# Transposing softmax blocks inside their own rows, and letting the value matmuls read them there

## The chip, the cores and the metric

The kernel runs on one core of one Trainium2 chip. The metric is the device time of one launch in microseconds; a kernel's figure is the median of its runs. The engines of the core go by the names of the profile: PE (TensorE matmuls) and PEld (its weight loads), DVE (VectorE), ACT (ScalarE), POOL (GpSimd), SP (SyncE, which issues the DMAs here).

## The reference

One residual layer of multi-query attention on 64 sequences ("images" below) of 128 tokens and 512 features, 16 heads of 64, one key and one value head shared by all. Everything is fp32.

```python
xn = layernorm(x, g_in)                                  # x: 64 x 128 x 512
q  = (xn @ Wq).reshape(b, n, 16, 64).transpose(0, 2, 1, 3) * 64 ** -0.5
k, v = split(xn @ Wkv)                                   # 64 wide each
k, v = [null_k; k], [null_v; v]                          # a null key in front: 129 keys
sim  = einsum('bhid,bjd->bhij', q, k) + bias             # bias 16 x 128 x 128
sim  = where(causal or masked, -max, sim)
attn = softmax(sim)
out  = einsum('bhij,bjd->bhid', attn, v)
out  = layernorm(out.reshape(b, n, 1024) @ Wo, g_out)
return x + out
```

## The kernel before

The work goes image by image (`b` from 0 to 63) in a software pipeline whose order is written out by hand: the order in the program is the order on each engine, and a step `n` runs parts of several images. Steps alternate between `step_a` (even `n`) and `step_b` (odd `n`); each ends with `region(n)`. Two steps make one round. The last five images go through `last_step` and `last_region`, which do the same with fewer parts.

**The softmax rows.** `S[b]` is one tile of 128 partitions by 8 slots by 194 words (`ROW = 1 + 64 + 128 + 1`). The 128 query rows of the 16 heads are folded by the causal mask: a partition quadrant of 32 rows holds, in each of its 8 slots, 64 columns for a query block that can see at most two key blocks of 32 (`LK`, columns 1 to 64) and 128 columns for one that can see up to four (`UK`, columns 65 to 192). Column 0 and column 193 belong to the null key. So the keys of each slot start at word 1 of a row of 194 words, an odd word in every slot.

An image's rows go through these operations, all of them in place in `S[b]`:

- `bias_add` (L526, POOL): allocates `S[b]` from the pool `sp` and writes bias plus mask, 1552 words a partition.
- `scores_add` (L573, DVE): adds the scores that PE left in PSUM (`heads`, L542).
- `scores_max` (L578, DVE), `exps` (L587, ACT), `rinv` (L604, DVE), `scale` (L608, POOL): the softmax of the two halves.
- `blocks_T` (L623, DVE): a transpose of the 32x32 blocks, 48 of them side by side on each quadrant, into the tile `sb` (6 blocks x 8 slots x 32 words, packed; one buffer in the pool `hp`).
- `values` (L654, PE): 32 matmuls, whose moving operand is read from `sb` and whose weights are the values `vr`. A matmul covers 32 rows and 64 output columns of the array, so eight of them (four quadrants by two column halves) fill it. Eight of the matmuls read two blocks of 4 slots (256 columns) and twenty-four read one (128 columns). In `sb` the 4 slots of a block lie behind one another: 128 words in one run.

fp32 matmuls appear in the profile as two records each, so an image has 64 records of L654.

**Who waits for whom around it.** With two buffers of `S`, `bias_add(n + 2)` takes the buffer of image `n`, whose last reader is `blocks_T(n)`, at the end of `region(n - 1)`. With one buffer of `sb`, `blocks_T(n + 1)` must come after `values(n)`. The order at the end of a step is

```python
    def region(n):
        ...            # scores_lower(nb), scores_one(nb, 1)            PE
        values(n)      #                                                PE
        ...            # scores_add, scores_max, scores_add             DVE
        values_out(n)  #                                                ACT
        blocks_T(n+1)  #                                                DVE
```

In `step_a` the next `bias_add` is the first thing on POOL after that; behind it in POOL's queue stand `pair_pow` (L784) and `scale` (L608). In `step_b` it comes late, behind `out_sums` and a `scale`.

The rest of PE's work in a step is the query projection (L488), the output projection (L738, L685) and the keys and values (L359); L488 and L738 are written as seven products of halves in place of eight.

Of the kernel before, what the change touches and what calls it, by code (L numbers as in the profile page):

```python
# [8 lines left out]
FP = mybir.dt.float32  # L9
# [8 lines left out]
def kernel(  # L18
# [59 lines left out]
    nc = tc.nc  # L78
# [3 lines left out]
    P = 128  # L82
# [7 lines left out]
    Q = 32  # L90
    NQ = P // Q
    NF = NC // 2
    R8 = 2 * NF
    NL = DH
    ROW = 1 + NL + N + 1
# [172 lines left out]
    mneg = const.tile([P, GB, ROW], FP, name="mneg")  # L268
    nc.gpsimd.memset(mneg[:, :, 0 : ROW : ROW - 1], 0.0)

    sp = ctx.enter_context(tc.tile_pool(name="sp", bufs=2))
    bp = ctx.enter_context(tc.tile_pool(name="bp", bufs=2))
    hp = ctx.enter_context(tc.tile_pool(name="hp", bufs=2))
    small = ctx.enter_context(tc.tile_pool(name="small", bufs=4))
# [237 lines left out]
    S, nmax, rsum = {}, {}, {}  # L512
# [106 lines left out]

    def blocks_T(b):  # L620

        sb = hp.tile([P, 6, R8, Q], FP, tag="sb", name=f"sb_{b}", bufs=1)
        nc.vector.transpose(  # L623
            sb.rearrange("p j e q -> p e j q"),
            S[b][:, :, 1 : ROW - 1].rearrange("p e (j k) -> p e j k", k=Q),
        )
        sbs[b] = sb

    pos = {}
# [221 lines left out]
    def region(n):  # L851
        nb, eb = n + 2, n + 1
        if nb < B:
            scores_lower(nb)
            scores_one(nb, 1)
        if n >= 0:
            values(n)
        if nb < B:
            scores_add(nb, 0)
            scores_max(nb, 0)  # L860
            scores_add(nb, 1)
            late_max.append(nb)
        if n >= 0:
            values_out(n)
        if 0 <= eb < B:
            blocks_T(eb)

    def last_region(n):
        nb, eb = n + 2, n + 1
        if nb < B:  # L870
            scores_one(nb, 0)
            scores_add(nb, 0)
        values(n)
        if nb < B:
            scores_max(nb, 0)
        values_out(n)
        if eb < B:
            blocks_T(eb)
        if nb < B:
            scores_one(nb, 1)  # L880
            scores_add(nb, 1)
            late_max.append(nb)
# [404 lines left out]
    q_half(7, 1)  # L1287
    weight_sum(3)
    blocks_T(0)
    for n in range(-1, P_LAST + 4):  # L1290
        step(n)
# [51 lines left out]
```

## Time and profile before

| | |
|---|---|
| Runs | 1071.23, 1072.93, 1073.17 us; median 1072.93 us |
| Span of the profiled execution | 1069.6 us |
| Busy, share of the span | PE 99%, PEld 83%, DVE 75%, POOL 65%, ACT 64% |
| Granted TensorE clock | 0.998 of full, mean over the span |

The profile gives the profiled execution by its span, from its first instruction to its last; no other time of that execution is listed. The median of the runs is 3.33 us more than this span, and the runs lie 1.6 to 3.6 us above it: what lies around the span (launch and end) is taken to be that, for both kernels. A line name such as L654 is a line of the kernel before. The changed kernel is two lines shorter from L624 on, so its L652 is L654 here.

### The profile page before, as it was taken

The page shows a single profiled execution, that of the slowest core. Times are in us where ns is not written, and L with a number is a line of the kernel's source. Part 1 is how long each engine was busy: PE and PEld are TensorE (multiplying, and loading weights), DVE is VectorE, ACT ScalarE, POOL GpSimd, SP SyncE. Part 2 cuts the span into 40 slices and gives each one's busy share as a digit, 9 for nine tenths or more (in the row PEclk, how much of TensorE's full clock was granted, in tenths as well). Part 3 has the DMA queues.
Part 4 walks back from the last instruction along what each step waited for, and adds up shares of the span by engine and source line. Part 5 has one row for each costly group of instructions (what it writes and reads, how often), then busy time and mean ns, then how long its engine had stood idle before and what let it go on. Part 6 is the DMA issues. An engine that isn't in the chain of part 4 may idle for free.

```text
span 1069.6 us, 31102 instructions
## 1 busy us (share of the span) xinstructions
PE 1055.3 (99%) x12272; PEld 883.4 (83%) x12272; DVE 806.0 (75%) x1676; ACT 679.3 (64%) x2748; POOL 695.3 (65%) x520
## 2 busy tenths in 40 slices
PE   8999999999999999999999999999999999999997
PEld 7877888888888888888888888888888888888653
DVE  5766787787878778787787877788787787666672
ACT  2565666676666666666766666766766766655682
POOL 3586667675775857667675775857667675765562
PEclk9999999999999999999999999999999999999999
DMA  6633414234241333314234141343313333101211
GB/s 209 168 107 93 131 49 129 73 102 139 75 124 52 129 105 102 118 48 135 83 103 139 53 138 57 107 130 99 113 54 125 94 103 120 50 32 46 66 61 70
DMA packets 68690, 105.11 MB, mean 98 GB/s; under 512 B 8640, under 2 KB 32832, under 8 KB 66752
## 3 DMA queue, kind: packets, MB, share of 16 engines
q1 hardware_dynamic: 67440, 102.08, 30.8%
q8 instruction: 96, 1.57, 0.7%
q10 hardware_dynamic: 1104, 1.05, 0.3%
q14 instruction: 50, 0.41, 0.1%
HBM read 67.45 MB, written 35.65 MB: 96 GB/s over the span
## 4 chain that ended last, share of the span: by engine, by line
PE 92%; DMA 4%; DVE 1%; ACT 1%; POOL 1%; issue 0%; SPq 0%; DVEq 0%; ACTq 0%
PE pa L488 19%; PE pyX L738 18%; PE pc L488 10%; PE pyY L738 9%; PE ps L542 9%; PE po L654 8%; PE pkv L359 6%; PE py L685 5%; PE pw L488 5%; PE pyw L738 4%; DMA x<-in_x_dram 2%; PE pq L437 1%; ACT oT L671 1%; DMA wq<-in_L_cond_Wq_dram 1%; DMA gin<-in_L_cond_g_in_dram 0%
## 5 line engine op out<-in xcount | busy, mean ns | idle before, releaser
L587 ACT ACTIVATE s<-s,nmax 128x65 f32<-128x65 f32 (+1 forms) x1024 | 372.0, 370 | 3.1 <-DVE nmax L578 3.1
L526 POOL TENSOR_TENSOR s<-biasp,mneg 128x1552 f32<-128x1552 f32 x64 | 206.1, 3221 | 159.8 <-DVE sb L623 151.9
L608 POOL TENSOR_TENSOR s<-s,rinv 128x512 f32<-128x512 f32 (+1 forms) x128 | 190.3, 1487 | 109.3 <-DVE rinv L604 109.3
L587 ACT ACTIVATION_READ_ACCUMULATOR s<-s,nmax 128x1 f32 x1024 | 198.2, 194 | 0.0
L671 ACT ACTIVATE oT<-po,nv 128x256 f32<-128x256 f32 x256 | 100.2, 474 | 153.9 <-PE po L654 153.8
L738 PE MATMUL pyX<-wT,oT 128*128 128x256 f32 x672 | 161.7, 383 | 0.0
L573 DVE TENSOR_TENSOR s<-ps,s 128x256 f32<-128x256 f32 (+2 forms) x188 | 125.1, 691 | 36.2 <-PE ps L542 36.2
L738 PEld LDWEIGHTS pyX<-wT,oT 128*128 128x128 f32 x672 | 123.5, 190 | 22.5 <-issue 2.7
L578 DVE TENSOR_REDUCE nmax<-s 128x8 f32<-128x520 f32 (+1 forms) x128 | 122.4, 956 | 2.4
L488 PE MATMUL pa<-xS,wq 128*128 128x256 f32 x480 | 123.2, 379 | 0.0
L623 DVE STREAM_TRANSPOSE sb<-s 128x1536 f32<-128x1536 f32 x64 | 113.3, 1770 | 4.7 <-POOL s L608 4.5
L542 PEld LDWEIGHTS ps<-kT,qT 64*64 64x64 f32 x4096 | 87.1, 134 | 26.2 <-issue 11.5
L542 PE MATMUL ps<-kT,qT 64*64 64x64 f32 (+1 forms) x4096 | 104.6, 248 | 1.5 <-DVE s L573 1.5
L488 PEld LDWEIGHTS pa<-xS,wq 128*128 128x128 f32 x480 | 91.2, 190 | 12.4
L654 PE MATMUL po<-sb,vr 32*64 32x128 f32 (+1 forms) x4096 | 91.3, 305 | 0.0
L654 PEld LDWEIGHTS po<-sb,vr 32*64 32x64 f32 x4096 | 70.8, 130 | 16.8 <-issue 10.7
L509 DVE TENSOR_TENSOR qT<-pc,ku 128x256 f32<-128x256 f32 x120 | 49.6, 413 | 42.5 <-ACT ku L499 31.6
L506 ACT COPY qT<-pa 128x256 f32<-128x256 f32 x60 | 22.3, 371 | 89.1 <-PE pa L488 89.1
L499 ACT COPY ku<-pa 128x256 f32<-128x256 f32 x120 | 44.7, 372 | 51.9 <-PE pa L488 50.0
L359 PE MATMUL pkv<-wkv,xT 128*128 128x128 f32 x512 | 71.8, 285 | 1.9 <-DVE kvt L374 1.9
L359 PEld LDWEIGHTS pkv<-wkv,xT 128*128 128x128 f32 x512 | 65.9, 195 | 8.7 <-issue 5.0
L718 POOL TENSOR_TENSOR yS<-oT 128x512 f32<-128x512 f32 x28 | 35.6, 1271 | 53.6 <-ACT oT L671 53.6
(95 smaller groups left out, 1957.2 us busy)
## 6 DMA issues: line engine op xcount, KB each, us to landing
x<-in_x_dram SPq DMA_DIRECT2D x64, 256.0 KB, 5.0
res<-in_x_dram SPq DMA_DIRECT2D x64, 256.0 KB, 6.2
out_dram<-y SPq DMA_DIRECT2D x64, 256.0 KB, 2.4
xd<-xb SPq DMA_DIRECT2D x14, 1024.0 KB, 4.0
xT<-xd SPq DMA_DIRECT2D x56, 256.0 KB, 5.9
vr<-vd SPq DMA_DIRECT2D x64, 128.0 KB, 2.7
kT<-kd SPq DMA_DIRECT2D x64, 64.0 KB, 1.9
kd<-kb SPq DMA_DIRECT2D x16, 128.0 KB, 2.6
```

The lines of the kernel that those rows point to most:

```text
L359: nc.tensor.matmul(pkv, xT[g][:, t, kc, :], wkv[:, kc, :], start=(kc == 0), stop=(kc == KC - 1),)
L488: nc.tensor.matmul(prod[tag], w[:, kc, f * P : (f + 1) * P], t[:, :, kc, :], start=(start and kc == 0), stop=(kc == HK - 1), skip_group_ch ...
L526: nc.gpsimd.tensor_tensor(S[b], biasp, mneg[:, t].unsqueeze(1).broadcast_to([P, R8, ROW]), ALU.add,)
L542: nc.tensor.matmul(to[r][i * DH : (i + 1) * DH, f, :], qT[g][rows, f, t, NQ - 1 - i if hf else i], kT[g][rows, 0 : NQ if hf else NQ // 2, ...
L573: nc.vector.tensor_tensor(sv, ps, sv, ALU.add)
L578: nc.vector.tensor_reduce(nmax[b][:, hf], S[b][:, :, WITH_NULL[hf]], AX.X, ALU.max, negate=True)
L587: nc.scalar.activation(row, row, AF.Exp, bias=nmax[b][:, hf, k : k + 1], accum_out=rsum[b][:, hf, k : k + 1],)
L608: nc.gpsimd.tensor_tensor(sv, sv, rinvs.pop((b, hf)).unsqueeze(2).broadcast_to([P, R8, sv.shape[2]]), ALU.mult,)
L623: nc.vector.transpose(sb.rearrange("p j e q -> p e j q"), S[b][:, :, 1 : ROW - 1].rearrange("p e (j k) -> p e j k", k=Q),)
L654: nc.tensor.matmul(po[s][rows, half], vr[g][quad(s), j, t, :], sb[quad(s), slots, r * NF : (r + 1) * NF, :], start=slots is first, stop=Tr ...
L671: nc.scalar.activation(oT[b][:, u * NF : (u + 1) * NF, :].rearrange("p f (i q) -> p i f q", i=NQ)[:, blocks], po, AF.Identity, bias=nv2,)
L738: nc.tensor.matmul(prod[key], h[:, c, :], w[:, c, :], start=(start and c == 0), stop=(c == HC - 1), skip_group_check=not start,)
```

## The change

The pool `sp` of softmax rows gets a third buffer. `blocks_T` transposes the blocks of `S[b]` onto themselves in place of writing them to `sb`, and `sbs[b]` is now a view of `S[b]` with its axes in the order that `values` expects. The tile `sb` is gone. `values` itself is the same text.

```diff
-    sp = ctx.enter_context(tc.tile_pool(name="sp", bufs=2))
+    sp = ctx.enter_context(tc.tile_pool(name="sp", bufs=3))
...
     def blocks_T(b):
 
-        sb = hp.tile([P, 6, R8, Q], FP, tag="sb", name=f"sb_{b}", bufs=1)
-        nc.vector.transpose(
-            sb.rearrange("p j e q -> p e j q"),
-            S[b][:, :, 1 : ROW - 1].rearrange("p e (j k) -> p e j k", k=Q),
-        )
+        blocks = S[b][:, :, 1 : ROW - 1].rearrange("p e (j k) -> p e j k", k=Q)
+        nc.vector.transpose(blocks, blocks)
+        sb = blocks.rearrange("p e j q -> p j e q")
         sbs[b] = sb
```

A partition holds 3 x 6208 = 18,624 bytes for these tiles afterwards; before it held 2 x 6208 + 6144 = 18,560.

In `values` the moving operand of a 128-column matmul was one run of 128 words. It is now four runs of 32 words, 194 words apart, each starting on an odd word. That of a 256-column matmul was two runs of 128 words and is now eight runs of 32. The number of matmuls, transposes and other operations, and their order on every engine, is the same. `bias_add(n + 2)` now takes the buffer of image `n - 1`, whose last reader is `values(n - 1)` on PE.

## The prediction

> **What bounds the kernel now.** I read the page first: the span, PE's line, the granted clock and the chain that ended last.
>
> ```profile
> span 1069.6 us, 31102 instructions
> PE 1055.3 (99%) x12272; PEld 883.4 (83%) x12272; DVE 806.0 (75%) x1676; ACT 679.3 (64%) x2748; POOL 695.3 (65%) x520
> PEclk9999999999999999999999999999999999999999
> PE 92%; DMA 4%; DVE 1%; ACT 1%; POOL 1%; issue 0%; SPq 0%; DVEq 0%; ACTq 0%
> ```
>
> PE is busy 1055.3 of 1069.6 us, at a clock that is not throttled, and the chain is PE for 92% of the span. A busy PE can hide slow matmuls, so I went on to the waits, taken by stage. The first transpose of blocks starts at 55.7 us (its row stands first below); behind it are PE's own waits from the windows up to 70 us (two), 70 to 200 (one), 200 to 500 (one) and from 980 us on (three). Between 500 and 980 us the view lists none for PE.
>
> ```profile
> L623 DVE STREAM_TRANSPOSE sb<-s x64: 1767/1769/1780, 55.7 to 1046.5; 128x1536 f32<-128x1536 f32 x64
> ```
>
> ```profile
> PE pc L488 <- DVE qT L509: 0.7, 1, 0.7
> PE pa L488 <- ACT qT L506: 0.5, 1, 0.5
> ...
> PE pa L488 <- ACT oT L671: 0.4, 1, 0.4
> ...
> PE pc L488 <- DVE qT L509: 0.4, 1, 0.4
> ...
> PE ps L542 <- DVE s L573: 1.5, 1, 1.5
> PE py L685 <- ACT oT L671: 0.6, 3, 0.2
> PE pa L488 <- ACT kp L499: 0.2, 1, 0.2
> ```
>
> They come to 4.3 us (columns: us in total, times, longest). So no wait that the change takes away can be worth more than 4.3 us, while what PE's own work gets longer is paid in full. The timeline of PE in a steady step shows the stretch that the change touches, with its neighbours (start, length, form, records):
>
> ```profile
> 503.70 1.57 PE L542 MATMUL ps<-kT,qT 64*64 64x64 f32 x64
> 505.20 1.42 PE L654 MATMUL po<-sb,vr 32*64 32x256 f32 x64
> 506.55 1.99 PE L738 MATMUL pyX<-wT,oT 128*128 128x256 f32 x8
> ```
>
> From start to start the values take 506.55 - 505.20 = 1.35 us an image, 64 x 1.35 = 86.4 us in all. That is the one PE term of the change.
>
> **The values read with the rows' stride (the term that decides).** Before, a 128-column matmul reads one run of 128 words; after, four runs of 32, at a step of 194 words, each from an odd word. No row shows PE reading from an odd word, so its price has to be bounded. A row shows runs of 32 at a step: the scores. Their moving operand is kT of the image, [4 blocks, 32], with a step of 128 words between blocks, the runs starting on a multiple of 32. Narrow windows of the timeline show how far apart sets of matmuls start:
>
> ```profile
> 504.65 0.51 PE L542 MATMUL ps<-kT,qT 64*64 64x128 f32 x12
> ...
> 504.98 0.29 PE L542 MATMUL ps<-kT,qT 64*64 64x128 f32 x4
> ...
> 505.46 0.49 PE L654 MATMUL po<-sb,vr 32*64 32x256 f32 x10
> 505.68 0.56 PE L654 MATMUL po<-sb,vr 32*64 32x128 f32 x21
> ...
> 506.24 0.38 PE L654 MATMUL po<-sb,vr 32*64 32x128 f32 x8
> ```
>
> One set of four score matmuls takes 0.29 us from start to end, three sets 0.51: a new set each (0.51 - 0.29) / 2 = 0.11 us, for 128 columns in four runs of 32. Of the values, a set of eight with 256 columns in two long runs starts at 505.46 and the next set at 505.68, so 0.22 us for 256 columns. 128 columns take 0.11 us either way: short runs at a step are read as fast as long runs, as long as they start on a multiple of 32 words. The 128-column sets go at the same pace: the one at 505.68 is the first of six, and the last eight records start from 506.24, (506.24 - 505.68) / 5 = 0.11 us a set. So the values are paced by the columns that go through the array, not by their weight loads, and what a run costs more would be seen in full. An image has 2 sets of 256 columns and 6 of 128, that is 2 x 8 + 6 x 4 = 40 runs of 32 one behind the other. Over 64 images, an extra d ns a run costs 64 x 40 x d = 2.56 us x d.
>
> The lower end is d = 0, the row of the scores. It can't go below that: the pace of 0.22 us / 256 = 0.86 ns a column is that of whole-array matmuls too, as the chain of waits has them (8 of 256 columns):
>
> ```profile
> 139.04 1.73 PE pyY L738 x8
> ```
>
> 1.73 us / 2048 = 0.84 ns, so a layout has no faster pace to go to. For the upper end I let each odd end of a run cost one column: two ends, and two column halves that read the same rows at once, so d = 4 x 0.86 = 3.4 ns and 2.56 x 3.4 = 8.7 us. I take d = 0, the value of the nearest row: it differs in the start of the run and in the step (128 words, not 194), while clock, pace and length of the runs are the same. The 256-column sets also get a third level (blocks, slots, words), of which no row shows a price. [...]
>
> **The transpose in place.** The same 64 instructions of 1536 words, now writing runs of 192 words from odd words.
>
> ```profile
> L331 DVE STREAM_TRANSPOSE xb<-x x56: 690/711/712, 59.4 to 886.1; 128x512 f32<-128x512 f32 x56
> ```
>
> ```profile
> DVE sb L623 <- POOL s L608: 4.5, 3, 2.0
> ```
>
> ```profile
> L573 DVE TENSOR_TENSOR s<-ps,s 128x1024 f32<-128x1024 f32 x64 | 77.7, 1214 | 0.0
> L573 DVE TENSOR_TENSOR s<-ps,s 128x256 f32<-128x256 f32 x120 | 44.7, 413 | 32.4 <-PE ps L542 32.4
> ```
>
> (In the first row stand the minimum, median and maximum ns of one, as in the row of L623 above; in the last two the busy us, the mean ns of one and the idle time before it with its releaser.) Transposes cost (1769 - 711) / 1024 = 1.03 ns a word, and L573, which reads and writes the same rows of S in place from their odd words, (1214 - 413) / 768 = 1.04 ns as well. So I take 1.77 us again and 0 for the change. It also loses a wait on PE (one buffer of sb): the view of the waits has it waiting for POOL alone, 4.5 us in three times, so that wait was never the late one and its loss gives 0.
>
> **The wait of the bias add.** This is where a long wait goes.
>
> ```profile
> POOL s L526 <- DVE sb L623: 151.9, 33, 6.3
> ...
> 508.88 3.23 POOL L526 TENSOR_TENSOR s<-biasp,mneg 128x1552 f32<-128x1552 f32 x1 [5.09 <-DVE sb L623]
> ...
> 505.90 1.22 DVE L573 TENSOR_TENSOR s<-ps,s 128x1024 f32<-128x1024 f32 x1
> 507.03 1.77 DVE L623 STREAM_TRANSPOSE sb<-s 128x1536 f32<-128x1536 f32 x1
> ```
>
> Before, the bias add waits for the transpose, 507.03 + 1.77 = 508.80. After, it waits for the values of the image before: 505.20 + 1.42 = 506.62. It starts about 2.2 us earlier in 33 steps. Queued behind it are the power (L784) and the scale (L608); they come up to 2.2 us earlier, until the reciprocal that the scale needs is the late one. PE waits for none of them in a steady step, so the gain is 0. In the other steps the bias add stands late in POOL's queue: only 33 of 64 waited for the transpose, and what it waits for now is over earlier than that, so the new wait costs 0 there. The bias add now runs beside the transpose and a score add. What it could do to them is shown by DVE operations that run beside POOL work, the transposes of L331 above and this one:
>
> ```profile
> L765 DVE TENSOR_TENSOR y<-kyp,kyp x28: 415/782/1480, 116.0 to 985.6; 128x256 f32<-128x256 f32 x28
> ```
>
> An add of two SBUF tiles is stretched up to 3.5 times; the transposes of L331 vary by 22 ns, those of L623 by 13. The two that move under the bias add have one SBUF operand each, so 0. The third buffer is 64 bytes a partition more, 0.
>
> **The sum.** 1069.6 + 0 + 0 + 0 = 1069.6 us of span; the median lies 3.33 us above it, which gives 1072.9 us, no change.
>
> **The rivals.**
>
> Slower, the odd starts (d > 0). For it: nothing in the trace shows PE at an odd word, and the values have no slack in their pace. Against: two streams a partition run at the pace of one, so the read side has room at least to double. With one column lost a run, d = 0.86, 2.2 us, 1075.1; with the full four columns 8.7 us, 1081.6. It decides from d = 0.8 ns a run, where 2.56 x 0.8 = 2.1 us. The values would take 1.35 + 40 x 0.86 = 1.38 us (one column) to 1.49 us.
>
> Faster, the freed POOL. If the 2.2 us of the bias add reach PE's waits at both ends, at most the 4.3 us above go: 1068.6. Against: the 1.5 us at the end hangs on a score add that stands in DVE's queue behind a reciprocal waiting for ACT, and the start's waits lie before or beside the first transposes, which stay where they are.
>
> Slower, the transpose itself, if writing onto what it reads doubled it to 3.5 us. DVE has about 25% of idle time, which is 4 us of a step of some 16 us, so most of it would be covered; were a sixth of the 1.77 us to come through (an assumption), 64 x 0.3 = 19 us, 1092. The L573 rows speak against it. It could also be that the third buffer changes nothing, the wait on DVE staying; then the time is the forecast's too.
>
> **How the numbers follow.** 0.2% is 2.1 us, about what a measurement of this kernel can tell from no change. No change (d below 0.8): 0.60. Odd starts with d of 0.8 or more: 0.26. Freed POOL by over 2.1 us: 0.10. The transpose: 0.04. So faster 0.10, same 0.60, slower 0.30. The range starts at 1070.0, two thirds of the freed POOL's most, and ends at 1079.0, d = 2.4; outside are some 0.05 below and 0.12 above.
>
> **What would show it.** Right: records of the values 1.35 us an image, sets 0.11 us apart; the transpose at 1.77 us; POOL's bias add released by PE with about 2.2 us less idle time in each of 33 steps, some 75 us of 151.9 left; PE at 99%. Wrong: the values longer than 1.38 us (odd starts); a transpose over 1.8 us; waits of PE on DVE between 500 and 980 us; or the 1.5 us wait of L542 at the end gone.

## The result: slower by a quarter of a percent, in the value matmuls

| | before | after |
|---|---|---|
| Median of 10 runs each | 1072.46 us (1070.28 to 1073.23) | 1074.36 us (1072.91 to 1075.97) |
| Ratio over all the runs | | 1.0025, 95% interval 1.0017 to 1.0033 |
| Span of the profiled execution | 1069.6 us | 1071.1 us |

The two medians alone are 1.90 us apart, a ratio of 1.0018; the ratio given with its interval is what is used below. The rival "odd starts" came nearest, not the forecast. From the page of the kernel after, the span, PE's line and the chain:

```profile
span 1071.1 us, 31062 instructions
PE 1055.2 (99%) x12272; PEld 881.3 (82%) x12272; DVE 806.5 (75%) x1676; ACT 679.3 (63%) x2748; POOL 696.8 (65%) x520
PE 94%; DMA 2%; DVE 1%; ACT 1%; POOL 1%; issue 0%; DVEq 0%; ACTq 0%
```

Nothing there gives the change away: PE is as busy as before and the chain is still PE. The timeline of PE in a steady step does (start, length, form, records; L652 and L736 are the L654 and L738 of before):

```profile
503.85 1.57 PE L542 MATMUL ps<-kT,qT 64*64 64x64 f32 x64
505.35 1.46 PE L652 MATMUL po<-s,vr 32*64 32x256 f32 x64
506.75 1.99 PE L736 MATMUL pyX<-wT,oT 128*128 128x256 f32 x8
```

The scores still take 1.50 us from start to start; the values take 1.40 where they took 1.35. From the starts of all records in the trace, the median image has 1.393 us in place of 1.350, and 64 x 0.043 = 2.75 us is 0.26% of the time. That is the whole loss, as far as the interval (0.17% to 0.33%) can tell. The groups of both forms of L652 grew (busy us, mean ns of one; 60.3 and 273, 44.5 and 400 before):

```profile
L652 PE MATMUL po<-s,vr 32*64 32x128 f32 x3072 | 61.6, 275 | 0.0
L652 PE MATMUL po<-s,vr 32*64 32x256 f32 x1024 | 46.0, 411 | 0.0
```

The spans of the two profiled executions differ by less, 1.5 us. A single execution scatters by more than a microsecond: the spans of the ten runs after go from 1071.1 to 1073.9 us. In the profiled execution of before, the granted clock was 0.57 from 20 to 24 us, where the one of after had 1.00. So the argument rests on PE's records and on the ratios of many runs, not on one span against another.

On the other engines the change went as it was meant to. The transpose's own row, then POOL and DVE in the same step:

```profile
L623 DVE STREAM_TRANSPOSE s<-s x64: 1766/1769/1780, 56.0 to 1048.0; 128x1536 f32<-128x1536 f32 x64
```

```profile
506.98 3.23 POOL L526 TENSOR_TENSOR s<-biasp,mneg 128x1552 f32<-128x1552 f32 x1 [3.04 <-PE po L652]
510.18 0.54 POOL L782 TENSOR_TENSOR rstdo<-rstdo,nhalf 128x1 f32<-128x1 f32 x1
512.18 1.05 POOL L608 TENSOR_TENSOR s<-s,rinv 128x512 f32<-128x512 f32 x1 [1.46 <-DVE rinv L604]
```

```profile
506.05 1.22 DVE L573 TENSOR_TENSOR s<-ps,s 128x1024 f32<-128x1024 f32 x1
507.19 1.77 DVE L623 STREAM_TRANSPOSE s<-s 128x1536 f32<-128x1536 f32 x1
```

The bias add starts at 506.98, 0.17 us after the values end, while the transpose that it used to wait for runs until 508.96. The transpose and the score add beside it are as long as before (1.77 and 1.22 us). The time that POOL gained became for the most part another wait, on the reciprocal; the waits of the kernel after, and the row of before that belongs to the second one:

```profile
POOL s L608 <- DVE rinv L604: 171.0, 89, 8.4
POOL s L526 <- PE po L652: 79.3, 29, 4.3
```

```profile
POOL s L608 <- DVE rinv L604: 109.3, 63, 7.6
```

151.9 us became 79.3, and 109.3 became 171.0: of 73 us less in the one wait, 62 came back in the other.

### The profile page after: what moved, and what is told of

Read it like the earlier page. It is cut to its first block, busy times and chain, and to the rows that moved or that the text cites. A ratio compares the mean times of both kernels' runs of the same rounds, so it can differ in the third digit from the quotient of the medians.

```text
span 1071.1 us, 31062 instructions
## 1 busy us (share of the span) xinstructions
PE 1055.2 (99%) x12272; PEld 881.3 (82%) x12272; DVE 806.5 (75%) x1676; ACT 679.3 (63%) x2748; POOL 696.8 (65%) x520
## 4 chain that ended last, share of the span: by engine, by line
PE 94%; DMA 2%; DVE 1%; ACT 1%; POOL 1%; issue 0%; DVEq 0%; ACTq 0%
PE pa L488 19%; PE pyX L736 18%; PE pc L488 10%; PE pyY L736 9%; PE ps L542 9%; PE po L652 8%; PE pkv L359 6%; PE py L683 5%; PE pw L488 5%; PE pyw L736 5%; DMA x<-in_x_dram 2%; PE pq L437 1%; ACT oT L669 1%; DVE st L284 0%; POOL s L608 0%
## 5 line engine op out<-in xcount | busy, mean ns | idle before, releaser
L608 POOL TENSOR_TENSOR s<-s,rinv 128x512 f32<-128x512 f32 (+1 forms) x128 | 190.0, 1485 | 172.6 <-DVE rinv L604 171.0
L526 POOL TENSOR_TENSOR s<-biasp,mneg 128x1552 f32<-128x1552 f32 x64 | 206.0, 3220 | 87.1 <-PE po L652 79.3
L736 PE MATMUL pyX<-wT,oT 128*128 128x256 f32 x672 | 161.7, 383 | 0.0
L736 PEld LDWEIGHTS pyX<-wT,oT 128*128 128x128 f32 x672 | 123.5, 190 | 22.8 <-issue 2.9
L623 DVE STREAM_TRANSPOSE s<-s 128x1536 f32<-128x1536 f32 x64 | 113.2, 1769 | 4.5 <-POOL s L608 4.5
L652 PE MATMUL po<-s,vr 32*64 32x128 f32 (+1 forms) x4096 | 94.2, 309 | 0.0
L652 PEld LDWEIGHTS po<-s,vr 32*64 32x64 f32 x4096 | 71.3, 129 | 18.6 <-issue 11.5
```

The source lines that it names most:

```text
L526: nc.gpsimd.tensor_tensor(S[b], biasp, mneg[:, t].unsqueeze(1).broadcast_to([P, R8, ROW]), ALU.add,)
L608: nc.gpsimd.tensor_tensor(sv, sv, rinvs.pop((b, hf)).unsqueeze(2).broadcast_to([P, R8, sv.shape[2]]), ALU.mult,)
L623: nc.vector.transpose(blocks, blocks)
L652: nc.tensor.matmul(po[s][rows, half], vr[g][quad(s), j, t, :], sb[quad(s), slots, r * NF : (r + 1) * NF, :], start=slots is first, stop=Tr ...
L736: nc.tensor.matmul(prod[key], h[:, c, :], w[:, c, :], start=(start and c == 0), stop=(c == HC - 1), skip_group_check=not start,)
```

## The experiments

Each kernel is named by what it does to the words that PE reads. "Values" is the median over 64 images of the time from the first value record to the first record after them, from the starts in the trace; it is 1.350 us before and 1.393 us after. A line, here and in the expectations, is a unit to count places by: four words, 16 bytes, with the tiles taken to start on a line. The place of a word in its line is its address in words modulo 4. What this unit is worth is for the runs to show. Where no time is given, the kernel was executed once, and only its records are used.

**First: is it the place, or the short runs themselves?** Three kernels are the changed one with the rows laid out wider, one is the kernel before with its packed tile spread.

```diff
 # keys_word4: (3, 200); keys_word2: (1, 196); keys_word1: (0, 196)
-        S[b] = sp.tile([P, R8, ROW], FP, tag="s", name=f"s_{b}")
+        S[b] = sp.tile([P, R8, 200], FP, tag="s", name=f"s_{b}")[:, :, 3 : 3 + ROW]
```

```diff
 # split36, on the kernel before
-        sb = hp.tile([P, 6, R8, Q], FP, tag="sb", name=f"sb_{b}", bufs=1)
+        sb = hp.tile([P, 6, R8, Q + 4], FP, tag="sb", name=f"sb_{b}", bufs=1)[:, :, :, 0:Q]
```

keys_word4: 

> In place as in the changed kernel, but a slot's keys start at word 4 of a row of 200 words: every run of 32 that PE reads starts on 16 bytes. A (a run pays for starting on an odd word): the values back to 1.350 us an image, time as before, ratio 1.000. B (a run pays for each 16-byte line that it cuts): 1.350 us too, ratio 1.000. C (a run pays for being short, for its step or for the third level, wherever it starts): 1.393 us, ratio 1.0025. Should the rest of the change cost or gain something (the bias add under the transpose, the rows in three buffers), the ratio is off 1.000 with the values at 1.350.

Measured: 1.349 us; 1070.00 against 1070.18 us, ratio 1.000 (0.9991 to 1.0008). The values of one image, from the timeline:

```profile
502.90 1.42 PE L652 MATMUL po<-s,vr 32*64 32x256 f32 x64
504.25 1.99 PE L736 MATMUL pyX<-wT,oT 128*128 128x256 f32 x8
```

keys_word2: 

> The same with the keys at word 2 of a row of 196 words: every run starts on 8 bytes and none on 16. A: the values 1.350 us an image, time as before. B: 1.393 us as in the changed kernel, or between, if a line of which two words are used costs less than one of which one is used; ratio 1.001 to 1.0025. C: 1.393 us.

Measured: 1.365 us; 1071.39 against 1070.18 us, ratio 1.0011 (1.0002 to 1.0020). 64 x 0.015 = 1.0 us fits.

```profile
502.99 1.43 PE L652 MATMUL po<-s,vr 32*64 32x256 f32 x64
504.36 1.99 PE L736 MATMUL pyX<-wT,oT 128*128 128x256 f32 x8
```

keys_word1: 

> The same with the keys at word 1 of a row of 196 words: odd as in the changed kernel, with another step between the slots. A, B and C: the values 1.393 us an image. If it was the step of 194 words that cost, 1.350 us.

Measured: 1.365 us, not the 1.393 that all three theories gave.

```profile
503.15 1.44 PE L652 MATMUL po<-s,vr 32*64 32x256 f32 x64
504.52 1.99 PE L736 MATMUL pyX<-wT,oT 128*128 128x256 f32 x8
```

split36: 

> The kernel before with its tile of transposed blocks spread: 32 words used of every 36, so that PE reads aligned runs of 32 at a step of 36 words, with three levels in the 256-column matmuls. A and B: the values 1.350 us an image. C: 1.393 us.

Measured: 1.350 us.

```profile
505.09 1.42 PE L654 MATMUL po<-sb,vr 32*64 32x256 f32 x64
506.44 2.00 PE L738 MATMUL pyX<-wT,oT 128*128 128x256 f32 x8
```

So C falls: runs of 32 at a step of 36 or of 200 words, with three levels, cost nothing when they start on 16 bytes (1.350 us in split36, 1.349 in keys_word4). The in-place transpose, the new wait and the third buffer together cost nothing that shows either (keys_word4, within 0.1%). A falls too: an even word (keys_word2, 1.365 us) costs what an odd one does (keys_word1, 1.365). And B doesn't explain why rows of 194 words cost three times what rows of 196 do at the same first word (0.043 and 0.015 us an image). Four words as the unit do fit: runs that start at multiples of four words, half of them not at multiples of eight, cost nothing (split36), and runs that start two words off such a multiple do (keys_word2).

**Second: a price by place, or by step?** With 194 words the starts of the slots alternate between words 1 and 3. Either word 3 is dear (D), or the step is (E).

```diff
 # keys_word3: [P, R8, 196] and [:, :, 2 : 2 + ROW], as above; rows194_word2:
+        S[b] = sp.tile([P, R8 * ROW + 2], FP, tag="s", name=f"s_{b}")[
+            :, 1 : 1 + R8 * ROW].rearrange("p (e c) -> p e c", e=R8)
 # kT_word3, on the kernel before (xT_word3 does the same to xT)
+        kT[g] = hp.tile([P, NQ * GB * Q + 4], FP, tag="kT", name=f"kT_{g}")[
+            :, 3 : 3 + NQ * GB * Q].rearrange("p (i t q) -> p i t q", i=NQ, t=GB)
```

keys_word3: 

> Keys at word 3 of a row of 196 words: every run of 32 starts on the last word of a 16-byte line. D (what a run costs goes by its place in the line: 0.4 ns at word 1 or 2, and 1.7 to 1.8 ns at word 3, since the changed kernel has half its runs at word 1 and half at word 3): the values 1.350 + 40 x 1.76 ns = 1.42 us an image, 64 x 0.07 = 4.5 us more in all, ratio 1.004. E (odd places cost 0.4 ns each, and the rest of the changed kernel's 43 ns comes from its step of 194 words, at which the slots lie differently in their lines): 1.365 us, ratio 1.001.

Measured: 1.367 us; 1071.15 against 1070.76 us, ratio 1.0002 (0.9993 to 1.0012). D falls by both; the time alone doesn't tell E's 1.001 from no change.

rows194_word2: 

> Rows of 194 words packed as in the changed kernel, but the whole tile moved by one word: half of the runs start at word 2 of a line, half on a line. D: the values 1.350 + 20 x 0.39 ns = 1.358 us an image. E: 1.36 to 1.39 us, since the step is kept.

Measured: 1.350 us, no cost at all, which neither D nor E gave: same step as the changed kernel, half the runs off a line.

```profile
503.53 1.42 PE L652 MATMUL po<-s,vr 32*64 32x256 f32 x64
504.88 1.99 PE L736 MATMUL pyX<-wT,oT 128*128 128x256 f32 x8
```

kT_word3: 

> The kernel before with kT, the moving operand of the scores, moved by three words: all its runs of 32 (48 in a row an image) start at word 3. D: the scores, 1.50 us an image from start to start, take 48 x 1.76 ns = 0.08 us more, 1.58 us; the values stay at 1.350 us. E: 48 x 0.4 ns = 0.02 us more. If only operands written by VectorE in place were slow: no change.

Measured: the scores 1.517 us for 1.501 (E's 0.02), the values 1.349. kT is written by DMAs, so it isn't a matter of VectorE having written the words in place.

```profile
503.17 1.59 PE L542 MATMUL ps<-kT,qT 64*64 64x64 f32 x64
504.69 1.42 PE L654 MATMUL po<-sb,vr 32*64 32x256 f32 x64
506.04 1.99 PE L738 MATMUL pyX<-wT,oT 128*128 128x256 f32 x8
```

xT_word3: 

> The kernel before with xT, the moving operand of the query projection, moved by three words: two runs of 128 a matmul, on the whole array, so one stream at a time. D, if a run's price is paid by the run: 2 x 1.76 = 3.5 ns a record more (216 to 219 or 220 ns). D, if it is paid by the line (one word of each line waits for the next line): 2 x 4 x 1.76 = 14 ns a record more. If it takes two streams on the same rows to be seen: 216 ns as before.

Measured: 217 ns a record for 216, in the products that read xT. The products behind them that read other tiles win a part of it back: sixteen records in succession, eight of them on xT, take 3459 ns for 3456. So a single stream on the whole array pays too, some 0.4 to 1 ns for its one step between runs, and not by the line.

**Third: the price of a step between two runs.** What orders all of these is the step from one run to the next inside a matmul: how many words are used of the last line of the one and the first line of the other. Call it w. In the changed kernel, a run that starts at word 1 uses one word of its last line; the next run starts at word 3 and uses one word of its first line, so w = 2 there. That w sets the price is theory G.

rows195_word1: 

> Rows of 195 words, keys at word 1: the runs of four slots start at words 1, 0, 3, 2 of a line, three of four not on a line. G: each change has 5 words in its two lines, so no cost, 1.350 us an image. H (only a line with one used word costs, and two such lines in succession most): each change has a line of one word or none, some 0.2 to 0.5 ns a run, 1.36 to 1.37 us.

Measured: 1.351 us, as G has it and H does not.

rows197_word1: 

> Rows of 197 words, keys at word 1: runs start at words 1, 2, 3, 0. The same starts as with 195 words, in the other order. G: of four changes two have 3 words in their two lines and two have 7, so two at some 1.5 ns, ten times an image: 1.350 + 0.03 = 1.38 us. H: no two lines of one word in succession, 1.36 to 1.37 us as with 195.

Measured: 1.375 us, between G's 1.38 and H's 1.36 to 1.37, nearer to G.

```profile
503.66 1.45 PE L652 MATMUL po<-s,vr 32*64 32x256 f32 x64
505.04 1.99 PE L736 MATMUL pyX<-wT,oT 128*128 128x256 f32 x8
```

The same four starts, in another order, cost 0.001 us with rows of 195 words and 0.025 us with rows of 197. So neither the starts nor the number of lines a run touches can be what counts; the neighbours are.

packed_odd, the kernel before with its packed tile one word further on:

```diff
-        sb = hp.tile([P, 6, R8, Q], FP, tag="sb", name=f"sb_{b}", bufs=1)
+        sb = hp.tile([P, 6 * R8 * Q + 1], FP, tag="sb", name=f"sb_{b}", bufs=1)
+        sb = sb[:, 1:].rearrange("p (j e q) -> p j e q", j=6, e=R8)
```

> The kernel before with its tile of transposed blocks moved by one word: runs of 128 words from odd words, 10 runs in a row an image in place of 40. G and H: the cost goes by the run and not by the word, 10 x 0.4 to 0.5 ns, 1.355 us an image. If a matmul paid for its odd words one by one, as much as with 40 runs at word 1 of 196: 1.365 us.

Measured: 1.350 us, less than expected.

```profile
502.17 1.42 PE L655 MATMUL po<-sb,vr 32*64 32x256 f32 x64
503.52 1.99 PE L739 MATMUL pyX<-wT,oT 128*128 128x256 f32 x8
```

I had counted the step from one matmul to the next as a step, 10 x 0.5 ns an image with the two inside; none of that showed (1.350 us, not 1.355). Inside the matmuls only the two sets of 256 columns have a step here, 2 an image.

Counting only steps inside a matmul, an image has 2 x 7 + 6 x 3 = 32. The table puts the kernels in order of w; the last column is the growth of the values over 1.350 us, divided by the steps at the least w:

| kernel | starts of four slots (word in line) | w of the steps | values, us | steps at the least w | ns a step |
|---|---|---|---|---|---|
| changed kernel | 1, 3, 1, 3 | 2 and 6 | 1.393 | 20 | 2.15 |
| rows197_word1 | 1, 2, 3, 0 | 3 and 7 | 1.375 | 20 | 1.25 |
| keys_word1, 2, 3 | all 1, all 2, all 3 | 4 | 1.365 to 1.367 | 32 | 0.5 |
| rows195_word1 | 1, 0, 3, 2 | 5 | 1.351 | 32 | 0 |
| rows194_word2 | 2, 0, 2, 0 | 6 | 1.350 | 32 | 0 |
| keys_word4, split36 | all 0 | 8 | 1.350 | 32 | 0 |

kT_word3 (w = 4, 32 steps an image, 0.016 us, 0.5 ns a step) falls on the same row.

The order by w is what the runs show; the sizes are less sharp. The starts of the sets of eight records inside an image show why. Before, the second set of 256 columns lasts 216 ns, a set of 128 columns 109, and one of these, the sixth set of the eight, 124. In the changed kernel they last 228, 114 to 115, and the sixth set 113: its pause of 15 ns is gone. So the growth of an image understates the price. By the sets that have no pause, a step costs 2.5 to 3 ns at w = 2 (228 - 216 for 4 steps), 1.5 at w = 3 (222 - 216 for 4) and about 0.6 at w = 4 (220 - 216 for 7). What sets these sizes stays open: no record shows how the read side fetches the words.

**Fourth: is that all of it?** rows194_word2 had the values back at 1.350 us, but its one execution took 1073.15 us against 1070.76, so I timed it.

rows194_word2_t: 

> The changed kernel with its tile of softmax rows moved by one word (rows of 194 words, keys at word 2), timed. G (a change from one run to the next costs by the words that are used in the two 16-byte lines on its sides: 2 words 2.5 to 3 ns, 4 words 0.4 to 0.5 ns, 5 or more nothing; here it is always 6): the values 1.350 us an image and the time of the kernel before, ratio 1.000, against 1.0025 of the changed kernel. If something else of the change costs, a ratio over 1.001.

Measured: 1074.08 against 1069.98 us, ratio 1.0038 (1.0024 to 1.0052), with the values at 1.349. This loss is of its own making. In both profiles of this kernel the first half's exponentials wait for the second half's score add, a wait that no other kernel here lists. I read it as a coarser dependency, from taking a view of one flat tile. Its waits, then PE in the tail, and the granted clock (the column after POOL's busy time) of a stretch there:

```profile
ACT s L587 <- DVE s L573: 8.0, 5, 2.8
```

```profile
1034.88 1.98 PE L542 MATMUL ps<-kT,qT 64*64 64x128 f32 x32 [3.17 <-DVE s L573]
1036.80 9.34 PE L683 MATMUL py<-wo,oT 128*128 128x512 f32 x16
```

```profile
1032.00:1040.00 8.00, 5.12 (x36) 3.09 (x37) 5.95 (x8) 5.21 (x23) 3.99 (x4) 0.65 0.20 66
```

The same two rows of the kernel before:

```profile
1035.50 1.10 PE L542 MATMUL ps<-kT,qT 64*64 64x128 f32 x32 [1.50 <-DVE s L573]
1036.54 7.13 PE L685 MATMUL py<-wo,oT 128*128 128x512 f32 x16
```

PE stands idle for 3.17 us (1.50 before), the clock granted over these 8 us is 0.65 (1.00 before), and 16 records of the output projection take 9.34 us (7.13 before). In the earlier execution of the same kernel the idle time was 3.16 us, the clock over the same 8 us 0.79, and the 16 records took 7.87 us. How the 4.1 us between the medians divide in the other executions isn't shown. The loss says nothing on the change, so a kernel without that wait was needed:

rows195_word1_t: 

> The kernel with rows of 195 words, keys at word 1, timed. G (all of the lost time is in the values, by the words in the lines on the two sides of a change from run to run): values 1.351 us an image, ratio 1.000 to 1.0005. If the transpose in place, the bias add released by PE, or the third buffer cost time too: the ratio stays above 1.001 with the values at 1.351.

Measured: 1070.15 against 1070.84 us, ratio 0.9991 (0.9982 to 1.0000), values 1.351 us.

```profile
503.78 1.42 PE L652 MATMUL po<-s,vr 32*64 32x256 f32 x64
505.14 1.99 PE L736 MATMUL pyX<-wT,oT 128*128 128x256 f32 x8
```

changed_again: 

> The changed kernel itself beside the one with rows of 195 words, on the same chip. G: 64 x (1.393 - 1.350) = 2.75 us more than the kernel before, ratio 1.0026. If the 1.0025 was a matter of the chip: 1.000.

Measured: 1073.32 against 1070.84 us, ratio 1.0023 (1.0014 to 1.0032), values 1.393 us. One word more to a row takes the whole loss away, on the same chip. Two things were not run: three buffers alone, and the change with two buffers, whose written order would, as I read it, wait on itself.

## Why the prediction was wrong

- **What bounds the kernel: right.** PE has no slack in the values: 2.75 us of longer matmuls came out as 2.7 us of time (0.0025 x 1072.46; 1.8 to 3.5 by the interval).
- **The step that failed is "I take d = 0".** In the terms of the sum, 2.56 us x d, it measured d = 2.75 / 2.56 = 1.08 ns a run, between the one column and the four of the bounds and above the 0.8 from which I said that the rival decides. But that is an average: the runs show that 20 steps an image are paid, those with w = 2 inside a matmul, and not 40 runs. I took the nearest row, the scores' kT, because length of the runs, clock and pace were the same. That row has every run on a line, and so it could not speak on the start of a run, the property that the change brings in. The argument that the read side "has room at least to double" failed too: xT_word3 pays with a single stream (217 ns a record for 216).
- **The rival was right in place, and by luck near in price.** It gave 1075.1 us for one column lost a run (1074.36 measured), but the reason that it gave isn't the one found. Odd starts were named; rows195_word1 has odd starts in two of four slots and costs nothing, keys_word2 has none and costs 0.5 ns a step. Nor is it the number of lines that a run touches: three of four runs touch nine lines in place of eight in rows195_word1 too, at 1.351 us. All prices here go by the place modulo four words, but no line by itself decides: lines with one used word cost nothing in rows195_word1, and lines with two cost 0.5 ns a step in keys_word2.
- **The transpose, the waits, the third buffer: right.** 1769 ns again; the bias add 506.98 - 503.85 = 3.13 us behind the start of the scores, where it was 508.88 - 503.70 = 5.18, so 2.05 us earlier (2.2 forecast). The wait left is 79.3 us; the "some 75" of the prediction was a slip, since 151.9 - 33 x 2.2 is 79.3. That the two agree to the tenth is chance, with 29 waits in place of 33. keys_word4 has all three together at 1.000.
- **The freed POOL: no gain, as forecast.** The wait at the end stayed, 1.5 us before and 1.3 after:

```profile
PE ps L542 <- DVE s L573: 1.3, 1, 1.3
```

- **The sum's time around the span was off**: 3.33 us for before, by a median; the profiled execution of the changed kernel took 1072.91 us with a span of 1071.1, 1.8 us, and over the ten runs after it is 1.8 to 3.0 us. It did no harm: the forecast came out as the median of before, with nothing added.

## What to carry to other kernels

Where PE is the bound, the access pattern of a moving operand is part of its time (1.350 or 1.393 us an image here). For fp32 runs of 32 words as here, look at each step between the runs of a matmul and keep at least five words in use over the two lines on its sides (with w never under 5 the values took 1.349 to 1.351 us; with a least w of 4, 3 and 2 they took 1.365 to 1.367, 1.375 and 1.393), or put every run on a line; one word of padding to a row did it here (1.351 us). When the nearest row of a trace differs in the very property that the change brings in, it gives no value for that property; weigh the rival's condition instead (here 0.8 ns a run, less than a column). And a busy share tells nothing of this: PE was at 99% with 1.350 us and with 1.393 us an image.

## What the runs showed of the hardware

- The same four starts of runs cost 0.001 or 0.025 us an image by their order alone (rows of 195 and of 197 words).
- Half of the runs off a line cost nothing (rows194_word2, 1.350 us), all of them off a line 0.5 ns a step (rows of 196 words), and half at word 1 and half at word 3 cost 2.15 ns at each of 20 steps of 32 by the growth of an image, 2.5 to 3 by the sets that have no pause (rows of 194 words).
- A step from one matmul to the next cost nothing (packed_odd, 1.350 us).
- VectorE's transpose took 1768 to 1770 ns and the large score add 1.21 to 1.22 us (means) before, after, and with rows of 194 (keys at word 2), 195, 196 (keys at words 2 and 3), 197 and 200 words; no price showed there.
- A pause of PE of 3.2 us in the tail, in place of 1.50, came with a granted clock of 0.65 over 8 us in one execution (rows194_word2_t) and 0.79 in another of the same kernel (rows194_word2); 16 records behind it took 9.34 and 7.87 us, in place of 7.13 at 1.00.
